# Four graph layers on one core: the last group's output projection by pairs, and a new order for its last full step

## The chip, the cores and the metric

The kernel runs on one core of a Trainium2 chip. The metric is the device time of one execution in microseconds. The core has TensorE (PE in the profile, with its weight loads as PEld), VectorE (DVE), ScalarE (ACT), GpSimd (POOL) and SyncE (SP), whose queue issues nearly all of the DMA transfers here.

## The reference

128 graphs of 64 nodes, each node with 512 features, pass through four layers. Each layer has the form `x = layernorm(x + f(x))`. All is float32.

```python
# layer 0: hypergraph convolution twice, with H = (adj != 0)
h = layer_norm(relu(hypergraph_conv(x, adj, W1, b1)), gamma, beta)      # 512 -> 1024
x = _layernorm(x + hypergraph_conv(h, adj, W2, b2) + x)                 # 1024 -> 512
# layer 1: additive attention weights A from s = x @ w @ a
x = _layernorm(x + A @ x @ w)
# layer 2: three graph convolutions  adj @ (x @ W) + b
x = _layernorm(x + gcn(relu(gcn(relu(gcn(x, W1, b1)), W2, b2)), W3, b3))
# layer 3: 8 heads of 64, softmax over the 64 nodes, plus adj and exp(-adj)
attn = softmax(q @ k.T * scale, masked) * 0.33 + 0.33 * adj + 0.33 * exp(-adj)
x = _layernorm(x + (attn @ v) @ W_out + b_out)
```

What follows concerns the end of layer 3: the softmax, `attn @ v`, the projection by `W_out`, and the last layer norm.

## The kernel before, in words

**Tiling.** Two graphs make a pair of 128 rows; four pairs make a group of 512 rows (`G = 4`), two pairs a duo. There are 16 groups (`NGRP`). A group's rows stay in the tile `x` (128 partitions, 4 pairs, 512 features) through all four layers.

**Products.** A product of 512x512 by 512x512 is done in blocks of 256 by Strassen's scheme in Winograd's form. `multiply` (L516) issues seven block products through `product` (L498), each four matmuls of 128x256, so 28 instead of 32. The left side is a `Left` object (L474), whose `sums` (L484) adds up four blocks on DVE; the right side needs seven blocks of the weight, three of them as given and four made once and kept in DRAM. `Stream` (L331) loads them through SP into a ring of 20 slots, one block at a time, in the order of use. Accumulators are `a_`, `b_` and `c_` with the name of the product; they, `pv` and the accumulators of plain products share four PSUM buffers. Between products ACT copies `u_` out (L524), or DVE adds the residual to it (L526), and DVE adds the results (L544, L548, L552); the last block is copied by ACT (L555) or added by DVE (L557).

**Plain products.** `rows_of` (L803), inside the first group's function, does it without Strassen: for one pair, eight matmuls of 128x256 into one accumulator.

**Layer 3** is the end of `second_half` (L980). `scores` (L1107) makes the dots `dot` and their scaled and masked form `sm`; `softmax` (L1140) works on `sm` in place, for each duo and each half `h2` of the heads: maximum, subtraction, exp on ACT, sum, reciprocal, multiplication. `turn_probs` (L1153) transposes `sm` into `ptp`, and adds the adjacency part to make `pt`. `attend` (L1175) multiplies by `v` into `pv`, which ACT copies into the left side `oT`. Then come `oT`'s sums, the product `wo`, `layer_norm` (L435) and the store. In the last group the norm and the store are made in two halves, of two pairs each.

**Order.** Three groups are in flight: the first half of one (`a`), the second half of the one before (`b`), and the tail of the one before that (`t`, from `v` on). Step by step, the list `order` (L1205) says which part is emitted next; a part that no group has at that step is left out. So step 16 has only `b` of group 15 and `t` of group 14, and step 17 only `t` of group 15:

```python
    order = """
        t.v1 a.c1 t.v b.gt t.soft a.w1a1 a.w1a t.soft2 a.resid b.l2a1 b.l2a a.w1b1 t.ptp a.w1b t.pv a.lnh t.osum
        b.l2b1 a.c2a b.l2b a.c2b b.gb3 load a.w21 b.gh a.w2 rows b.l2c1 b.l2c2 a.ss b.l2c t.o1 a.den t.o2 a.c3 b.agg t.o
        a.p1 b.xT a.p2 b.q1 b.q t.ln3 b.k1 prep b.k b.dots
    """.split()
```

A trailing digit is a stop inside a product (`v1` is after its third block product, `o1` after the first, `o2` after the third). `gt` is the graph product ahead of layer 2, `l2a`, `l2b`, `l2c` are layer 2's products, `agg` its last aggregation, `xT` the transposes `xtp` ahead of layer 3.

A scheduler then orders each engine's instructions, and may move one ahead of others that were written before it. Two things bind it. `behind(key)` (L471) keeps instructions after a given addition on DVE. And an `Engine` wrapper (L119) puts each instruction after the one written before it on the same engine, while `opening[0]` is true, which it is in the first group's list `start` only.

Of the kernel before, what the change touches and what calls it, by code (L numbers as in the profile page):

```python
# [8 lines left out]
FP = mybir.dt.float32  # L9
U8 = mybir.dt.uint8  # L10
AF = mybir.ActivationFunctionType
ALU = mybir.AluOpType
AX = mybir.AxisListType

P = 128
C = 64
D = 512
DH = 1024
HEADS = 8
G = 4  # L20
T = G * P
KD = D // P
Q = 256
# [18 lines left out]
def kernel(  # L42
# [71 lines left out]
    PE, DVE, ACT, POOL, SP = (  # L114
        getattr(mybir.EngineType, n) for n in ("PE", "DVE", "Activation", "Pool", "SP")
    )
    opening = [False]

    class Engine:  # L119

# [3 lines left out]

        def __getattr__(self, name):
            op = getattr(self.engine, name)
            if not opening[0]:
                return op

            def call(*args, **kwargs):  # L130
                with in_turn(self.kind):
                    return op(*args, **kwargs)

            return call
# [90 lines left out]
    class Weight:  # L225
# [17 lines left out]
                nc.sync.dma_start(out=t, in_=self.kept[u][what])  # L243
            return t

        def load_quads(self):
            quads = []
            for u in range(self.halves):
                b = {}
                for k, n in ((0, 0), (1, 0), (0, 1), (1, 1)):  # L250
                    b[k, n] = self.tile(f"b{k}{n}", 0, u)
                    nc.sync.dma_start(out=b[k, n], in_=self.quad_src(u, k, n))
                quads.append(b)
            return quads
# [76 lines left out]
    class Stream:  # L331


        def __init__(self, uses):
            self.todo = []
            for wt, q in uses:
                if q == 0:
                    self.todo.append((wt, q, None, 8))
                else:
                    self.todo += [(wt, q, what, wt.halves) for what in ORDER]  # L340
            self.here = {}
            self.held = 0
            self.to_make = {}
            self.uses = uses

        def pump(self):
            while self.todo and self.held + self.todo[0][3] <= RING:
                wt, q, what, n = self.todo.pop(0)
                self.held += n
                if q > 0:  # L350
                    self.here[wt, q, what] = [wt.load(q, what, u) for u in range(wt.halves)]
                elif wt in by_pairs:
                    by_pairs[wt] = None if wt.scaled else wt.load_quads()
                else:
                    self.to_make[wt] = wt.load_quads()
# [65 lines left out]
    def bcast(t, n):  # L421

        return t.unsqueeze(2).to_broadcast([P, n, C])
# [47 lines left out]
    def behind(key):  # L471
        return tc.issue_after(last_add[key]) if key in last_add else nullcontext()
# [25 lines left out]
    def product(acc, lefts, wt_q, what, first, last, flipped):  # L498
        ws = stream.take(*wt_q, what)
        n_k = 2 * len(lefts)  # L500
        for blk in range(2):
            for i in range(n_k):
                left, wt = lefts[i // 2].left[what][:, i % 2], ws[i // 2][:, i % 2]
                if flipped:
                    lhsT, rhs = wt[:, blk * P : (blk + 1) * P], left
                else:
                    lhsT, rhs = left[:, blk * P : (blk + 1) * P], wt

                ten.matmul(  # L509
                    acc[:, blk, :], lhsT, rhs,  # L510
                    start=(first and blk == 0 and i == 0), stop=(last and i == n_k - 1),
                    skip_group_check=True,
                )
        stream.done(*wt_q, what)

    def multiply(lefts, wt_q, dst, key, flipped=False, res=None, stops=(3,)):  # L516


        acc = [ps_acc.tile([P, 2, Q], FP, name=f"{n}_{key}", tag="acc") for n in "ab"]

        def snap(ps, m, n, what):
            t = work.tile([P, 2, Q], FP, name=f"{what}_{key}", tag="w")
            if res is None:
                act.copy(t, ps)  # L524
            else:
                vec.tensor_add(t, ps, res(m, n))  # L526
            return t

        pa, pc = acc
        product(pa, lefts, wt_q, B11, True, False, flipped)  # L530
        s1 = snap(pa, 0, 0, "u1")
        if 1 in stops:
            yield
        product(pc, lefts, wt_q, T1, True, False, flipped)
        s5 = snap(pc, 1, 1, "u5")
        if 2 in stops:
            yield
        product(pa, lefts, wt_q, T2, False, False, flipped)
        s2 = snap(pa, 0, 1, "u2")
        if 3 in stops:  # L540
            yield
        pb = ps_acc.tile([P, 2, Q], FP, name=f"c_{key}", tag="acc")
        product(pb, lefts, wt_q, B21, True, True, flipped)
        vec.tensor_add(dst(0, 0), pb, s1)  # L544
        if 4 in stops:
            yield
        product(pa, lefts, wt_q, T3, False, False, flipped)
        vec.tensor_add(dst(1, 1), pa, s5)  # L548
        if 5 in stops:
            yield  # L550
        product(pc, lefts, wt_q, B22, False, True, flipped)
        last_add[key] = vec.tensor_add(dst(0, 1), pc, s2).ins  # L552
        product(pa, lefts, wt_q, T4, False, True, flipped)
        if res is None:
            act.copy(dst(1, 0), pa)  # L555
        else:
            vec.tensor_add(dst(1, 0), pa, res(1, 0))  # L557

    def whole(gen):
        for _ in gen:  # L560
            pass

    def nat(t):

        return lambda m, n: t[:, 2 * m : 2 * m + 2, n * Q : (n + 1) * Q]
# [225 lines left out]
    def constant(g):  # L791
        for p in range(G):
            vec.scalar_tensor_tensor(
                g["x"][:, p, :], bw_bc, g["cs"][:, p : p + 1], g["x"][:, p, :], ALU.mult, ALU.add
            )

    def first_group(g):


        q, xg = g["q"], g["x"]  # L800
        pair = lambda p: xg[:, p, :]

        def rows_of(p, ts, quads, u0=0, u1=None, ps=None):  # L803

            if ps is None:
                ps = ps_acc.tile([P, 2, Q], FP, name=f"pp_{p}", tag="acc")
            us = range(len(ts))[u0:u1]
            for n in range(2):
                for u in us:
                    for c in range(KD):  # L810
                        ten.matmul(
                            ps[:, n, :], ts[u][:, c, p * P : (p + 1) * P], quads[u][c // 2, n][:, c % 2],
                            start=(n == 0 and u == 0 and c == 0), stop=(u == len(ts) - 1 and c == KD - 1),
                            skip_group_check=True,
                        )
            return ps

        def stats(mv, st, at, src):
            vec.bn_stats(st, src)
# [160 lines left out]
    def second_half(g):  # L980
# [94 lines left out]
        probs = [scores(g, duo, qT, kT) for duo in range(2)]  # L1075
        yield "dots"
        v = big.tile([P, G, D], FP, name=f"v_{q}", tag="big")
        for _ in multiply([left], (w_v, q), nat(v), f"v_{q}"):
            yield "v1"
        yield "v"  # L1080
# [1 line left out]
        with behind(f"v_{q}"):  # L1082
            softmax(g, 1, probs[1], (0,))
        yield "soft"
        with behind(f"l0w10_{q + 2}"):
            softmax(g, 1, probs[1], (1,))
        yield "soft2"
        pts = [turn_probs(g, duo, probs[duo]) for duo in range(2)]
# [9 lines left out]
        yield "o"  # L1098
        with behind(f"q_{q + 1}"):
            o = out[q * T : (q + 1) * T, :].rearrange("(p t) d -> t p d", t=P)  # L1100
            for pairs in (range(G),) if q < NGRP - 1 else (range(2), range(2, G)):
                layer_norm(xg, f"l3_{q}_{pairs[0]}", pairs)
                at = slice(pairs[0], pairs[-1] + 1)
                nc.sync.dma_start(out=o[:, at], in_=xg[:, at])
        yield "ln3"

    def scores(g, duo, qT, kT):  # L1107

# [29 lines left out]
        return ds  # L1138

    def softmax(g, duo, ds, h2s):  # L1140

        for h2 in h2s:
            d, key = ds[h2], f"{g['q']}_{duo}_{h2}"
            mx = small.tile([P, 8], FP, name=f"mx_{key}", tag="mx")
            vec.reduce_max(mx, d, axis=AX.X)
            vec.tensor_sub(d, d, bcast(mx, 8))
            act.activation(d, d, AF.Exp)
            sm = small.tile([P, 8], FP, name=f"sum_{key}", tag="sum")
            vec.reduce_sum(sm, d, axis=AX.X)
            vec.reciprocal(sm, sm)  # L1150
            vec.tensor_mul(d, d, bcast(sm, 8))

    def turn_probs(g, duo, probs):  # L1153

# [20 lines left out]
    def attend(g, duo, pts, v, left):  # L1175
# [36 lines left out]
        b.l2a1 b.l2a a.lnh b.l2b1 a.c2a b.l2b a.c2b b.gb3 load a.w21 b.gh a.w2 b.l2c1 sumsq b.l2c2 a.ss b.l2c a.den b.agg  # L1212
        a.c3 a.p1 b.xT sumsk a.p2 b.q1 b.q b.k1 rows b.k prep b.dots
    """.split()
    lag = {"a": 0, "b": 1, "t": 2}
    todo = []
    for what in start:
# [6 lines left out]
            todo.append((what, 0, None))  # L1224
    n_start = len(todo)
    for step in range(1, NGRP + 2):
        for what in order if step > 1 else step_1:
            who, dot, name = what.partition(".")
            key = (who, step - lag[who], name) if dot else (what, step + 1, None)
            if 0 <= key[1] < NGRP and key not in todo:  # L1230
                todo.append(key)
    used = {
        ("a", "w1a"): w_1[0], ("a", "w1b"): w_1[1], ("a", "w2"): w_2, ("a", "p2"): w_l1, ("b", "l2a"): w_g[0],
        ("b", "l2b"): w_g[1], ("b", "l2c"): w_g[2], ("b", "q"): w_q, ("b", "k"): w_k, ("t", "v"): w_v,
# [6 lines left out]
        if wt is not None:  # L1241
            uses.append((wt, q))
    stream = Stream(uses)
    opening[0] = True
    groups, gens, preps = {0: first}, {}, {0: prepare(first)}
    next(preps[0])
    next(preps[0])
# [3 lines left out]
        w_2.load_raw()  # L1251
    scaling, bw_parts = w_2.scale(), w_2.beta_times()
    for n, (who, q, name) in enumerate(todo):
        opening[0] = n < n_start
        if who == "load":
            if q > 1:
                groups[q] = load_group(q)
# [98 lines left out]
```

## Time and profile before

| | us |
|---|---|
| median of three runs (2805.82 to 2807.02) | 2805.87 |
| the profiled execution | 2804.13 |
| its span, first to last instruction | 2802.3 |
| PE busy | 2769.3 (99%) |
| DVE busy | 2003.7 (72%) |
| ACT busy | 818.2 (29%) |
| step 16, from group 14's `dot` to group 15's | 2651.84 to 2758.06 |
| last group's `v` begins | 2760.09 |
| last matmul begins, end of its modelled run | 2793.3, 2793.68 |

The granted TensorE clock is 0.999 over the whole span. Matmuls are pipelined and their ends are modelled, so starts say more than durations; a busy PE is not a PE at its peak. The profiled execution lies 1.74 us under the median. In a row of the timeline, the time in brackets is what the engine stood idle before, with what ended the wait.

### The profile page before, as it was taken

What the parts mean: (1) busy time and instruction counts of PE and PEld (TensorE: products, weight loads), DVE (VectorE), ACT (ScalarE), POOL (GpSimd) and SP (SyncE); (2) the same over time, 40 slices, a digit from 0 to 9 for tenths busy, and PEclk for the clock granted to TensorE, in tenths of its full rate; (3) what the DMA queues carried; (4) which work ended last, traced back from release to release, by engine and by line L of the source; (5) the groups of instructions that cost most, each with busy time, mean ns of one, the idle gap of its engine ahead of it and who ended that gap; (6) DMA issues with size and microseconds to landing.
All of it is one profiled execution on the core that took longest, in us unless ns stands there. A gap on an engine that the chain in (4) does not pass through costs nothing.

```text
span 2802.3 us, 67764 instructions
## 1 busy us (share of the span) xinstructions
PE 2769.3 (99%) x28862; PEld 2362.0 (84%) x28862; DVE 2003.7 (72%) x3861; ACT 818.2 (29%) x1467; POOL 38.1 (1%) x72
## 2 busy tenths in 40 slices
PE   9999999999999999999999999999999999999998
PEld 7878888888888888888888888888888888888877
DVE  6768677676776767767677776767767677676756
ACT  3223323232232322322233232232323223232222
POOL 2000000000000000000000000000000000000000
PEclk9999999999999999999999999999999999999999
DMA  8444454454544545445454454545545454454541
GB/s 259 165 127 148 130 158 140 139 162 131 165 129 136 163 129 166 127 142 163 133 158 130 142 160 128 162 129 150 152 133 162 130 158 135 132 162 129 147 118 64
DMA packets 309660, 405.94 MB, mean 145 GB/s; under 512 B 57424, under 2 KB 184944, under 8 KB 309360
## 3 DMA queue, kind: packets, MB, share of 16 engines
q1 hardware_dynamic: 304384, 385.84, 46.5%
q0 software_dynamic: 4976, 15.76, 1.5%
q8 instruction: 229, 3.75, 0.5%
q14 instruction: 71, 0.58, 0.1%
HBM read 370.57 MB, written 30.93 MB: 143 GB/s over the span
## 4 chain that ended last, share of the span: by engine, by line
PE 86%; DVE 8%; ACT 1%; issue 0%; DVEq 0%
PE a_l0w L509 13%; PE b_l0w L509 7%; PE a_l2b L509 4%; PE a_q L509 4%; PE a_k L509 4%; PE a_v L509 4%; PE c_l0w L509 4%; PE a_l2a L509 4%; PE a_l1w L509 4%; PE gt_l L458 3%; PE a_wo L509 3%; PE a_l2c L509 2%; PE gt_l0h L458 2%; PE b_l1w L509 2%; PE b_v L509 2%; PE b_l2b L509 2%
## 5 line engine op out<-in xcount | busy, mean ns | idle before, releaser
L509 PE MATMUL a_l0w<-w2w,aT_l0h 128*128 128x256 f32 x720 | 164.3, 381 | 0.0
L440 DVE BATCH_NORM_STATS2 st_l<-x 128x6 f32<-128x512 f32 x248 | 160.2, 674 | 0.1
L509 PEld LDWEIGHTS a_l0w<-w2w,aT_l0h 128*128 128x128 f32 x720 | 135.6, 190 | 18.8
L696 ACT ACTIVATE h<-h 128x1024 f32<-128x1024 f32 x58 | 61.3, 1057 | 216.6 <-DVE h L552 195.0
L444 DVE TENSOR_SCALAR x<-x,mv_l,rs_l 128x512 f32<-128x512 f32 x248 | 120.1, 542 | 1.8
L466 ACT COPY aT_l<-gt_l 128x512 f32<-128x512 f32 x176 | 90.5, 600 | 71.1 <-PE gt_l L458 71.0
L509 PE MATMUL b_l0w<-w2w,s_l0h 128*128 128x256 f32 x480 | 108.5, 379 | 0.0
L509 PEld LDWEIGHTS b_l0w<-w2w,s_l0h 128*128 128x128 f32 x480 | 90.1, 190 | 13.5
L1023 ACT ACTIVATE aT_h<-gth,gb_col 128x256 f32<-128x256 f32 x128 | 48.4, 489 | 159.0 <-PE gth L1015 159.0
L431 ACT ACTIVATE rs_l<-mv_l,eps_t 128x4 f32<-128x4 f32 (+1 forms) x63 | 18.8, 298 | 258.1 <-DVE mv_l L441 256.8
L509 PE MATMUL a_l2b<-gwbw,aT_h 128*128 128x256 f32 x360 | 86.9, 384 | 4.7 <-ACT aT_oT L1195 4.7
L509 PE MATMUL a_l2a<-aT_l,gwaw 128*128 128x256 f32 x360 | 86.6, 383 | 1.0 <-ACT aT_l L466 1.0
L509 PE MATMUL a_q<-aT_xT,wqw 128*128 128x256 f32 x360 | 86.6, 383 | 0.2 <-ACT aT_xT L1062 0.2
L509 PE MATMUL a_v<-wvw,aT_xT 128*128 128x256 f32 x360 | 86.6, 383 | 0.0
L509 PE MATMUL a_l2c<-gwcw,aT_h 128*128 128x256 f32 x360 | 85.3, 380 | 0.6 <-DVE g L548 0.6
L509 PE MATMUL a_wo<-wow,aT_oT 128*128 128x256 f32 x360 | 85.3, 380 | 0.0
L509 PE MATMUL a_l1w<-ww,aT_l 128*128 128x256 f32 x360 | 85.1, 379 | 0.0
L509 PE MATMUL a_k<-aT_xT,wkw 128*128 128x256 f32 x360 | 85.0, 379 | 0.0
L509 PE MATMUL a_l0w<-w1aw,aT_l 128*128 128x256 f32 x336 | 82.3, 388 | 0.0
L509 PE MATMUL a_l0w<-w1bw,aT_l 128*128 128x256 f32 x336 | 81.7, 379 | 0.0
L526 DVE TENSOR_TENSOR u_l0w<-a_l0w,b_bc 128x512 f32<-128x512 f32 x56 | 38.5, 688 | 59.8 <-PE a_l0w L509 59.8
L509 PEld LDWEIGHTS a_l2b<-gwbw,aT_h 128*128 128x128 f32 x360 | 67.1, 190 | 15.2 <-ACT aT_oT L1195 6.6
(503 smaller groups left out, 6464.5 us busy)
## 6 DMA issues: line engine op xcount, KB each, us to landing
w2w<-w2k SPq DMA_DIRECT2D x210, 256.0 KB, 2.7
x<-in_x_dram SPq DMA_DIRECT2D x15, 1024.0 KB, 6.3
w1aw<-w1ak SPq DMA_DIRECT2D x60, 256.0 KB, 2.7
w1bw<-w1bk SPq DMA_DIRECT2D x60, 256.0 KB, 2.7
ww<-wk SPq DMA_DIRECT2D x60, 256.0 KB, 2.7
gwaw<-gwak SPq DMA_DIRECT2D x60, 256.0 KB, 3.7
gwbw<-gwbk SPq DMA_DIRECT2D x60, 256.0 KB, 2.7
gwcw<-gwck SPq DMA_DIRECT2D x60, 256.0 KB, 2.7
```

The lines of the kernel that those rows point to most:

```text
L431: act.activation(rs[:, at], mv[:, at, 1], AF.Sqrt, bias=eps_t)
L440: vec.bn_stats(st, xg[:, p, :])
L444: vec.tensor_scalar(xg[:, p, :], xg[:, p, :], mv[:, p, 0:1], rs[:, p : p + 1], ALU.subtract, ALU.mult)
L458: ten.matmul(ps[g][f * C : (f + 1) * C, c, p, :], src(2 * duo + p)[rows, c0 : c0 + C], mat[rows, 2 * duo + p, :], start=True, stop=True,)
L466: act.copy(o[:, :, :, g, :], ps[g])
L509: ten.matmul(acc[:, blk, :], lhsT, rhs, start=(first and blk == 0 and i == 0), stop=(last and i == n_k - 1), skip_group_check=True,)
L526: vec.tensor_add(t, ps, res(m, n))
L696: act.activation(hn, hn, AF.Relu)
L1023: act.activation(o[:, :, h, :], ps[h][:, c].rearrange("p (d a) i -> p d (a i)", d=2), AF.Relu, bias=gb2_col[:, k : k + 1],)
```

## The change

**The last full step.** Step 16 gets a list of its own, `step_last`, and step 17 another, `rest_last`. In `step_last`, `b.gt` stands between the two parts of `t.v`, `t.ptp` between the two parts of `b.l2a`, and `b.agg` ahead of `t.o2`. The second half of the softmax of group 14 is kept behind the last addition of its `v`.

**The last group.** `last_rows` takes the place of the tail for group 15. The projection is plain, with `rows_of` moved outward so that both can call it, and with the four given blocks of `W_out`, loaded together. Each pair is added to `x`, normalised and stored by itself; the last pair is added in two half rows, each with its statistics. `ptp` of duo 0 goes ahead of the seventh block product of `v`; `pv` of duo 0, the projection of pair 0, `ptp` of duo 1, half of pair 1, `pv` of duo 1, the other half, and pairs 2 and 3 follow. The softmax is split into `softmax_steps` and issued in written order. From the last group's `v` on, PE and DVE keep the written order (`strict`); ACT does not.

```diff
@@ Stream
                 if q == 0:
                     self.todo.append((wt, q, None, 8))
+                elif (wt, q) == (w_o, NGRP - 1):
+                    self.todo.append((wt, q, None, 4))
...
-                if q > 0:
+                if what is None and q > 0:
+                    self.here[wt, q] = wt.load_quads(q)
+                elif q > 0:
@@ multiply
         last_add[key] = vec.tensor_add(dst(0, 1), pc, s2).ins
+        if 6 in stops:
+            yield
         product(pa, lefts, wt_q, T4, False, True, flipped)
@@ second_half
         v = big.tile([P, G, D], FP, name=f"v_{q}", tag="big")
+        if q == NGRP - 1:
+            yield from last_rows(g, probs, v, left)
+            return
...
-        with behind(f"l0w10_{q + 2}"):
+        with behind(f"l0w10_{q + 2}" if q < NGRP - 2 else f"v_{q}"):
             softmax(g, 1, probs[1], (1,))
...
-            for pairs in (range(G),) if q < NGRP - 1 else (range(2), range(2, G)):
-                layer_norm(xg, f"l3_{q}_{pairs[0]}", pairs)
-                at = slice(pairs[0], pairs[-1] + 1)
-                nc.sync.dma_start(out=o[:, at], in_=xg[:, at])
+            layer_norm(xg, f"l3_{q}")
+            nc.sync.dma_start(out=o, in_=xg)
         yield "ln3"
+
+    def last_rows(g, probs, v, left):
+
+        q, xg = g["q"], g["x"]
+        o = out[q * T : (q + 1) * T, :].rearrange("(p t) d -> t p d", t=P)
+        gen = multiply([left], (w_v, q), nat(v), f"v_{q}", stops=(3, 6))
+        next(gen)
+        yield "v1"
+        steps = [[softmax_steps(g, duo, probs[duo], h2) for h2 in range(2)] for duo in range(2)]
+        for n in range(2):
+            for h2 in range(2):
+                next(steps[0][h2])
+        for n in range(2):
+            next(steps[1][0])
+        for h2 in range(2):
+            next(steps[0][h2])
+        next(gen)
+        yield "v2"
+        left = Left(f"oT_{q}")
+        pts = turn_probs(g, 0, probs[0])
+        whole(gen)
+        yield "v"
+        attend(g, 0, pts, v, left)
+        for n in range(2):
+            next(steps[1][1])
+        for h2 in range(2):
+            next(steps[1][h2])
+        yield "pv0"
+
+        def projected(p, ps=None, n=None):
+            return rows_of(p, [left.t], stream.here[w_o, q], ps=ps, ns=range(2) if n is None else (n,))
+
+        def added(p, ps, n=None):
+            cols = slice(0, D) if n is None else slice(n * Q, (n + 1) * Q)
+            row = xg[:, p, cols]
+            vec.tensor_add(row, ps.rearrange("p n f -> p (n f)")[:, cols], row)
+
+        def written(p):
+            layer_norm(xg, f"l3_{q}_{p}", (p,))
+            nc.sync.dma_start(out=o[:, p], in_=xg[:, p])
+
+        ps = projected(0)
+        pts = turn_probs(g, 1, probs[1])
+        added(0, ps)
+        written(0)
+        yield "o1"
+        ps = projected(1, n=0)
+        attend(g, 1, pts, v, left)
+        ps = projected(1, ps, n=1)
+        added(1, ps)
+        written(1)
+        yield "pv1"
+        added(2, projected(2))
+        written(2)
+
+        st = small.tile([P, 2, 6], FP, name="st_last", tag="st_last", bufs=1)
+        ps = None
+        for n in range(2):
+            ps = projected(3, ps, n=n)
+            added(3, ps, n)
+            vec.bn_stats(st[:, n], xg[:, 3, n * Q : (n + 1) * Q])
+        mv = small.tile([P, 1, 2], FP, name="mv_last", tag="mv_last", bufs=1)
+        vec.bn_aggr(mv[:, 0, :], st.rearrange("p n s -> p (n s)"))
+        rs = rstd(mv, 1, "last")
+        vec.tensor_scalar(xg[:, 3], xg[:, 3], mv[:, 0, 0:1], rs[:, 0:1], ALU.subtract, ALU.mult)
+        nc.sync.dma_start(out=o[:, 3], in_=xg[:, 3])
+        yield "o"
+
+    def softmax_steps(g, duo, ds, h2):
+
+        d, key = ds[h2], f"{g['q']}_{duo}_{h2}"
+        mx = small.tile([P, 8], FP, name=f"mx_{key}", tag="mx")
+        vec.reduce_max(mx, d, axis=AX.X)
+        yield
+        vec.tensor_sub(d, d, bcast(mx, 8))
+        act.activation(d, d, AF.Exp)
+        yield
+        sm = small.tile([P, 8], FP, name=f"sum_{key}", tag="sum")
+        vec.reduce_sum(sm, d, axis=AX.X)
+        vec.reciprocal(sm, sm)
+        vec.tensor_mul(d, d, bcast(sm, 8))
+        yield
@@ the lists of steps
+    step_last = """
+        t.v1 b.gt t.v t.soft t.soft2 b.l2a1 t.ptp b.l2a t.pv t.osum b.l2b1 b.l2b b.gb3 b.gh b.l2c1 b.l2c2 b.l2c t.o1 b.agg
+        t.o2 t.o b.xT b.q1 b.q t.ln3 b.k1 b.k b.dots
+    """.split()
+    rest_last = "t.v1 t.v2 t.v t.pv0 t.o1 t.pv1 t.o".split()
+    orders = {1: step_1, NGRP: step_last, NGRP + 1: rest_last}
...
+        if n == n_start:
+            strict.clear()
+        if n == n_end:
+            strict.update((PE, DVE))
```

More of the change, by code (lines that the diff above doesn't have):

```diff
@@ L116 @@
     )
-    opening = [False]
+    strict = set()
     class Engine:
@@ L126, in __getattr__ @@
             op = getattr(self.engine, name)
-            if not opening[0]:
+            if self.kind not in strict:
                 return op
@@ L244, in load, with load_quads @@
             return t
-        def load_quads(self):
+        def load_quads(self, q=0):
             quads = []
@@ L250, in load_quads @@
                 for k, n in ((0, 0), (1, 0), (0, 1), (1, 1)):
-                    b[k, n] = self.tile(f"b{k}{n}", 0, u)
+                    b[k, n] = self.tile(f"b{k}{n}", q, u)
                     nc.sync.dma_start(out=b[k, n], in_=self.quad_src(u, k, n))
@@ L795, in constant, with rows_of @@
             )
+    def rows_of(p, ts, quads, u0=0, u1=None, ps=None, ns=range(2)):
+        if ps is None:
+            ps = ps_acc.tile([P, 2, Q], FP, name=f"pp_{p}", tag="acc")
+        us = range(len(ts))[u0:u1]
+        for n in ns:
+            for u in us:
+                for c in range(KD):
+                    ten.matmul(
+                        ps[:, n, :], ts[u][:, c, p * P : (p + 1) * P], quads[u][c // 2, n][:, c % 2],
+                        start=(n == 0 and u == 0 and c == 0), stop=(u == len(ts) - 1 and c == KD - 1),
+                        skip_group_check=True,
+                    )
+        return ps
     def first_group(g):
@@ L801, in first_group @@
         pair = lambda p: xg[:, p, :]
[L803 to L816, printed above, removed]
         def stats(mv, st, at, src):
@@ L1142, in softmax @@
         for h2 in h2s:
[L1143 to L1151, printed above, removed]
+            whole(softmax_steps(g, duo, ds, h2))
     def turn_probs(g, duo, probs):
@@ L1226 @@
     for step in range(1, NGRP + 2):
-        for what in order if step > 1 else step_1:
+        for what in orders.get(step, order):
             who, dot, name = what.partition(".")
@@ L1231 @@
                 todo.append(key)
+    n_end = todo.index(("t", NGRP - 1, "v1"))
     used = {
@@ L1243 @@
     stream = Stream(uses)
-    opening[0] = True
+    strict.update((PE, DVE, ACT))
     groups, gens, preps = {0: first}, {}, {0: prepare(first)}
@@ L1253 @@
     for n, (who, q, name) in enumerate(todo):
-        opening[0] = n < n_start
+        if n == n_start:
+            strict.clear()
+        if n == n_end:
+            strict.update((PE, DVE))
         if who == "load":
```

## The prediction

> **What bounds the kernel now.** I read the page first. One row says who is the bound over the whole span:
>
> ```profile
> PE 2769.3 (99%) x28862; PEld 2362.0 (84%) x28862; DVE 2003.7 (72%) x3861; ACT 818.2 (29%) x1467; POOL 38.1 (1%) x72
> ```
>
> TensorE is busy 99%. A change gains only where TensorE stands still, or after its last matmul. The instruction orders of the two kernels are the same, names aside, up to step 16 (the last in which two groups overlap), so all that counts lies after about 2650 us. For that stretch I read the chain of waits; each piece that is not PE is time in which TensorE had nothing to do:
>
> ```profile
> 2668.27 0.97 ACT aT_l L466 x2
> ...
> 2687.37 0.61 DVE pt L1169
> ...
> 2731.37 0.47 DVE x L444
> ...
> 2771.44 1.19 DVE mx L1145 x2
> ...
> 2792.71 1.29 DVE st_l L440 x2
> ...
> 2797.33 0.55 DVE x L444
> ```
>
> Five holes: the evictions of gt_l before l2a; the pt additions that hold pv; the layer norm that holds the transposes xtp; the second softmax (from mx) in the last group; and the whole norm at the end. The timeline of PE gives the places, and what TensorE waited for in brackets:
>
> ```profile
> 2669.28 1.99 PE L509 MATMUL a_l2a<-aT_l,gwaw 128*128 128x256 f32 x8 [1.04 <-ACT aT_l L466]
> ...
> 2731.88 1.57 PE L1057 MATMUL xtp<-identc,x 64*128 64x64 f32 x30 [1.03 <-DVE x L444]
> ...
> 2776.51 1.29 PE L1162 MATMUL ptp<-identc,sm 64*128 64x64 f32 x16 [1.67 <-DVE sm L1151]
> 2777.73 3.17 PE L1186 MATMUL pv<-pt,v 64*64 64x64 f32 x120
> ```
>
> A product of four matmuls (x8: two records each) starts every 1.727 us; a block of 128 records of 64x64 takes 2.02 us (dot, 2758.06 to 2760.09). So pv at 3.17 us for 120 is slow. The granted clock in half-microseconds says why:
>
> ```profile
> 2776.50:2777.00 0.50, 0.46 (x8) 0.32 (x8) 0.50 (x2) 0.00 (x0) 0.00 (x0) 1.00 0.00 0
> 2777.00:2777.50 0.50, 0.39 (x8) 0.39 (x8) 0.50 (x2) 0.00 (x0) 0.00 (x0) 0.50 0.00 0
> ```
>
> The column before the DMA share is the clock: it halves at 2777.0, after 3.4 us in which TensorE was almost idle, and comes back at about 2780.4. Last, the stores, in the list of DMA issues (size and time to landing):
>
> ```profile
> out_dram<-x SPq DMA_DIRECT2D x1, 1024.0 KB, 4.2
> out_dram<-x SPq DMA_DIRECT2D x2, 512.0 KB, 2.9
> ```
>
> **The change, step 16.** From dot at 2651.84 to dot at 2758.06, before takes 106.2 us.
>
> (a) gt goes from behind v to between v's third and fourth product. The work is the same 2.02 us with one way in and out of small tiles as before, but its four copies on ACT (2.03 us) and the four sums on DVE (4 x 0.6) now run under four products. l2a starts directly: 1.0 us gained. What goes late is the second half of the softmax: v's last add moves from 2664.53 to about 2666.75, so sm is ready at about 2673.3.
>
> (b) The 32 transposes ptp go into l2a after its third product, due 2673.5, so sm just makes it. Slack 0.2 us; each 0.1 us that DVE is later costs as much. The pt additions (4 x 0.6 us) then run under l2a's second half. Before, PE took from the end of l2a (2681.88) to b_l2b (2689.54) for ptp, pv and one product of l2b: 7.66 us. After: l2a ends at 2681.8, now with ptp inside. pv still waits for a PSUM slot, freed by the copy of a_l2a on ACT, which stands behind two relu of 0.66 us: 2682.85. Then 2.02 + 0.1 for pv, 1.83 for the first product of l2b, so b_l2b at 2686.88 against 2689.54. With (a) that is 2.66 us, my figure up to here.
>
> (c) agg goes ahead two products of wo. It waits for nothing (g is written 0.6 us into a_wo). It puts 4 additions and the norm of group 15 on DVE 3.45 us earlier; ending at about 2726.5 against TensorE's arrival at 2727.7, they no longer hold xtp (1.03 us), nor its first copies. The wait of the last product on x L548 (0.2) goes too, but u_wo, now behind the norm's work on DVE, holds the fourth product for about 0.2. Sum: a_q at 2729.65 against 2733.69, or **4.0 us** for the step. Groups 14 and 15 use the same weights in the same order; the SP queue is unchanged but for wo's loads, four instead of seven, waiting for four free slots at once: at about 2747 instead of 2737 to 2748, and needed 28 us later. They stand ahead of group 14's store, whose data are ready at 2752.5. Cost nothing; were they 28 us late, every microsecond more would count.
>
> **The change, last group.** I keep the old clock, as if v began at 2760.09.
>
> Work: wo by pairs is 32 matmuls of 128x256 instead of 28: 4 x 0.432 = 1.73 us more on TensorE. Six more ways in and out of small tiles at about 0.1 (a_v after dot is 1.83 and not 1.73): 0.6 more. Against that the Strassen sums (4 x 0.6) and three u_wo leave DVE.
>
> The chain in the written order: sum_01 waits for its exp until 2766.87, mul ends 2768.5; v's adds follow their products to 2771.46. ptp0 runs at 2770.64 (0.6), v's last product to 2773.1, its copy on ACT to 2773.95. pv0 2774.0 to 2775.15 (hole 0.9); its copies, two in 1.09, to 2776.28 (hole 1.2). DVE meanwhile: pt0, then the rest of softmax 1, ending at 2777.1. pp0 2776.3 to 2779.9; ptp1 to 2780.55; half of pp1 to 2782.4; pv1 (pt1 at 2782.0) to 2783.6; the other half to 2785.43. Here is the added wait: on ACT the square root of pair 0 stands ahead of pv1's copies. It waits for x<-pp0, which on DVE stands behind pt1: add 2781.9, statistics 0.72, aggregate 0.17, root to 2783.8, copies to 2784.95. pp2 needs them at 2785.43, so 0.5 us spare. pp2 to 2788.9, pp3 to 2792.35, last result at 2792.5; before, 2793.68.
>
> After that: DVE adds half a row (128x256: the 0.42 of L654's shape; bounds 0.2 and 0.69), statistics of it 0.4 (no row; between 0.17 of an aggregate and 0.67 of the full row), aggregate 0.2, root 0.3, reciprocal 0.15, scale 0.55, with gaps: the last scale ends at 2794.85. Before, the scale of 2797.33 is the first of two (1.00 us together) and ends the work at 2798.33: 3.5 us later. The store: 256 KB instead of 512, with nothing queued ahead. 1024 and 512 KB land in 4.2 and 2.9, so 1.3 for 512 KB, and 256 KB by the line 2.25 (upper bound 2.7, the page's median for w2w loads of that size, in traffic). Gain 0.65, bounds 0.2 and 1.0. Tail: 3.5 + 0.7 = **4.2 us**.
>
> [...] between 2773.1 and 2777.0 before did 0.34 + 0.46 us of matmuls. The trace dipped all the same, at some 24% busy. After, the worst 3.4 us (2772.9 to 2776.3) is some 38% busy. [...] by the row's measure a dip is possible[...], and 3.4 us at half speed under pp0 cost 1.7, leaving 6.5. I take no dip, as step 16 has stretches of 67% without one[...].
>
> **Sum.** 4.0 + 4.2 = 8.2 us. The profiled execution took 2804.13 (span 2802.3 and 1.8 around it), so 2795.9 for such a one; the median 2805.87 stands 1.74 higher and goes to **2797.7**.
>
> **The rivals.**
> Main case, 0.60: its own range 2796.0 to 2799.5, from the store's bounds (0.5 each way), the slack of 0.2 at ptp, and switches at 0 to 0.2 each.
> Dip of 3.4 us in the last group, 0.18: 2799.4. For it, the trace's dip at 24%; against, 38% and more.
> One half doesn't pay, 0.17: the gaps of step 16 return elsewhere (softmax 1 late at ptp, u_wo late at T3), or strict order makes DVE or ACT late by the 0.2 and 0.5 us of slack and more. Against: DVE's chain per pair (add, statistics, aggregate, root, reciprocal, scale) is 2.95 us against 3.45 of matmuls. Time: 2805.87 - 4.1 = 2801.8, which is within 0.2%.
> Slower, 0.03: the clock halves at pp0 and stays low to the end. From 2776.3 on there are 15.4 us of matmuls; at half speed each low microsecond costs 0.5, so 16 us of low clock eat the 8.2. All of it low: 2805.87 - 8.2 + 15.4 x 1.0 = 2813. Against: [...] pp is dense.
> The change doesn't do what it says, 0.02: the orders show the moves on each engine as described, so only a delayed wo load could undo it.
>
> 0.2% is 5.6 us, about what a measurement of this kernel can tell from no change. Faster by more: main and dip, and part of the third, 0.82; within: 0.14; slower by more: 0.04. The range reaches from the main case's better end, with a store at its best bound, to the third case: 2795.4 to 2801.9.
>
> **What would show it.** Right: a_l2a directly after v's seventh product; xtp without a wait; a_q about 4 us earlier against the first dot; in the tail holes of about 0.9 and 1.2 before pv0 and pp0, none before pp2; last matmul to end of span about 5.6 us instead of 8.6; clock 1.00 throughout the last group. Wrong: a clock of 0.50 under pp0, pp2 waiting for ACT's copies of pv1, ptp waiting for sm in l2a, or a last store that lands no sooner than 2.9 us.

## The result, and the profile after

The changed kernel takes 2797.61 us (median of seven runs, 2796.10 to 2800.23) against 2806.66 us before (seven runs, 2805.82 to 2807.03): a ratio of 0.997, 95% interval 0.9958 to 0.9982. The three runs of before that stood ahead of the prediction are among the seven. The profiled execution of the changed kernel took 2797.61 us, with a span of 2795.8.

The page's row of busy times is as good as unchanged. TensorE has eight records more (the four matmuls of the plain projection at two records each, 28870 against 28862), and what was gained is idle time:

```profile
PE 2769.4 (99%) x28870; PEld 2362.2 (84%) x28870; DVE 2000.2 (72%) x3858; ACT 818.3 (29%) x1469; POOL 38.1 (1%) x72
```

The chain of waits from 2640 us on shows which of the five holes are left. Columns: start, length, engine, what.

```profile
2669.74 1.73 PE a_l2a L513 x8
...
2685.38 0.49 ACT aT_oT L1275
...
2728.85 0.69 PE xtp L1063 x12
...
2771.63 0.98 ACT aT_oT L1275 x2
...
2787.64 0.89 DVE x L132 x2
2788.53 0.04 issue
2788.58 2.01 PE pp L132 x8
...
2792.30 0.55 DVE x L132
```

Before l2a and before xtp the chain now runs on PE without a break: the copies of gt_l and the norm of group 15 are off it. At 2685.38 the copies of pv appear where the additions of pt stood. At 2771.63 it is the copies of the first pv, where the second softmax stood. New is 2787.64: DVE's work on rows `x`, and after it a part of the projection `pp`. The timeline of PE says what that is:

```profile
2685.91 1.99 PE L513 MATMUL a_l2b<-gwbw,aT_h 128*128 128x256 f32 x8 [0.69 <-ACT aT_oT L1275]
...
2728.78 1.22 PE L1063 MATMUL xtp<-identc,x 64*128 64x64 f32 x32
...
2770.18 1.16 PE L132 MATMUL pv<-pt,v 64*64 64x64 f32 x64
2772.65 3.72 PE L132 MATMUL pp<-wob,aT_oT 128*128 128x256 f32 x16 [1.31 <-ACT aT_oT L1275]
...
2779.96 7.17 PE L132 MATMUL pp<-wob,aT_oT 128*128 128x256 f32 x32
2788.58 1.99 PE L132 MATMUL pp<-wob,aT_oT 128*128 128x256 f32 x8 [1.44 <-DVE x L132]
```

xtp has no wait in front. In the last group there is one hole of 1.31 us before pair 0's projection (`pp` at 2772.65), and one of 1.44 before the last four matmuls, which wait for DVE. The second is not in the prediction.

The clock (the column before the DMA share) stays at 1.00 to the last matmul, and a block of 64 records of pv takes 1.16 us. The row below is a stretch of 3.4 us around the first of these holes, and none around it has less than its 2.09 us of work on TensorE. Around the second hole, at the very end of the matmuls, a stretch of 3.4 us still holds 1.96:

```profile
2770.90:2774.30 3.40, 2.09 (x40) 1.77 (x32) 3.04 (x7) 2.88 (x4) 0.00 (x0) 1.00 0.00 0
```

The stores of one pair each, in the list of DMA issues from 2785 us on, land in 2.0 us, against 2.9 for two pairs:

```profile
out_dram<-x SPq DMA_DIRECT2D x3, 256.0 KB, 2.0
```

Where the time came from can be read off the starts in the timeline of PE, in one execution each. All in us; dot is that of group 14 at first, and v the last group's:

| stretch | before | after | gain |
|---|---|---|---|
| start of the span to group 14's dot | 2651.84 | 2653.14 | -1.30 |
| dot to a_l2a | 17.44 | 16.44 | 1.00 |
| a_l2a to b_l2b | 20.26 | 18.16 | 2.10 |
| b_l2b to a_q | 44.15 | 42.92 | 1.23 |
| a_q to group 15's dot | 24.37 | 24.37 | 0 |
| dot to v | 2.03 | 2.02 | 0.01 |
| v to the end of the span | 42.21 | 38.75 | 3.46 |

From group 14's dot on the change gains 7.8 us. All but 0.07 of the last group's 3.46 comes behind its last matmul, whose modelled end is 33.59 us after v's start in before and 33.52 in after; from there to the end of the span it is 8.62 and 5.23.

The first row has nothing to do with the change: the instruction orders are the same up to there, and the difference is there already at the first gt_l0h (44.00 and 45.39 us). It fits the clock at the start. The first 64 records of `pp` take 14.08 us in before and 15.01 in after, the next 64 take 13.98 in both, and the trace's first record of the full clock begins at 12.2 us in before and at 15.1 in after. Over the twelve profiled executions of this study group 14's dot starts between 2651.84 and 2654.48, so what lies ahead of it moves a run by 2.6 us. That is why all experiments below are read by stretches first, and by medians second.

### The profile page after: what moved, and what is told of

It is laid out like the page before. It is cut to its first block, busy times and chain, and to the rows that moved or that the text cites. A ratio compares the mean times of both kernels' runs of the same rounds, so it can differ in the third digit from the quotient of the medians.

```text
span 2795.8 us, 67769 instructions
## 1 busy us (share of the span) xinstructions
PE 2769.4 (99%) x28870; PEld 2362.2 (84%) x28870; DVE 2000.2 (72%) x3858; ACT 818.3 (29%) x1469; POOL 38.1 (1%) x72
## 4 chain that ended last, share of the span: by engine, by line
PE 86%; DVE 7%; issue 4%; ACT 1%; DMA 1%; POOL 0%; SPq 0%; DVEq 0%; POOLq 0%
PE a_l0w L513 13%; PE b_l0w L513 7%; PE a_l2b L513 4%; PE a_q L513 4%; PE a_k L513 4%; PE a_v L513 4%; PE c_l0w L513 4%; PE a_l2a L513 4%; PE a_l1w L513 4%; PE gt_l L462 3%; PE a_wo L513 3%; PE a_l2c L513 2%; PE gt_l0h L462 2%; PE b_l1w L513 2%; PE b_l2b L513 2%
## 5 line engine op out<-in xcount | busy, mean ns | idle before, releaser
L513 PE MATMUL a_v<-wvw,aT_xT 128*128 128x256 f32 x336 | 80.8, 383 | 0.0
L513 PE MATMUL a_wo<-wow,aT_oT 128*128 128x256 f32 x336 | 79.5, 379 | 0.1
```

What stands on the lines that cost most here:

```text
L513: ten.matmul(acc[:, blk, :], lhsT, rhs, start=(first and blk == 0 and i == 0), stop=(last and i == n_k - 1), skip_group_check=True,)
```

## The experiments

**Each half by itself.** e1_step_only keeps step 16's list and has the last group as before; e2_tail_only keeps the last group's new tail and has step 16 as before.

```diff
 e1_step_only, against the changed kernel
-        if q == NGRP - 1:
-            yield from last_rows(g, probs, v, left)
-            return
...
-    orders = {1: step_1, NGRP: step_last, NGRP + 1: rest_last}
+    orders = {1: step_1, NGRP: step_last}
...
-        if n == n_end:
-            strict.update((PE, DVE))
...
 e2_tail_only, against the changed kernel
-        with behind(f"l0w10_{q + 2}" if q < NGRP - 2 else f"v_{q}"):
+        with behind(f"l0w10_{q + 2}"):
...
-    orders = {1: step_1, NGRP: step_last, NGRP + 1: rest_last}
+    orders = {1: step_1, NGRP + 1: rest_last}
```

> Only step 16's new order; the last group as before (Strassen projection, norm and store in two halves, scheduler's order). Theory: the two halves of the change add up without touching each other. Step 16, from dot to dot, takes 101.9 us as in the changed kernel (106.2 before), and from the last group's v to the end 42.2 us as before; so about 4.3 us faster than before, near 2802.3. Rival, the halves depend on each other (what step 16 saves comes back as a later weight load or a late norm in the last group): v to the end over 43 us, total gain under 3. Rival, the gain of the change is in the opening of the run: dot of group 14 starts more than 2 us earlier here and step 16 is near 106.

> Only the last group's new tail; step 16 in the old order. Theory: v to the end of the span takes 38.75 us as in the changed kernel (42.2 before), step 16 106.2 as before; about 3.5 us faster than before, near 2803.2. Rival, the halves depend on each other: v to the end differs from 38.75 by more than 0.5 us.

Measured: e1 2801.55 us, ratio to before 0.9985 (0.9979 to 0.9992); e2 2802.37 us, ratio 0.9987 (0.9980 to 0.9993). These are medians of 21 runs each, and before, run beside them 41 times, took 2805.81: gains of 4.26 and 3.44 us, 7.70 together, which agrees with the 7.8 of the traces. Step 16 takes 101.90 in e1 and 106.24 in e2; v to the end 42.66 and 38.84. So the halves add up: each stretch has its new length with its own half of the change and its old one without. The rival, that one half gives back what the other gains, falls, and so does the one that puts the gain into the opening: in e1 dot of group 14 starts at 2653.92, later than before.

e1 also shows the old tail's clock once more. The row below is the 3.4 us ahead of its drop, in stretches of the same kind as above; the next is a stretch after it:

```profile
2769.55:2772.95 3.40, 1.64 (x27) 1.00 (x26) 3.40 (x7) 1.82 (x3) 0.00 (x0) 1.00 0.00 0
...
2775.00:2777.00 2.00, 2.00 (x64) 1.88 (x68) 1.70 (x3) 0.00 (x0) 0.00 (x0) 0.50 0.04 8
```

The clock fell to 0.50 with TensorE 48% busy in the 3.40 us ahead, and stayed there for 6.8 us, against 3.4 in before. Of the five runs with the old tail, e1 and e7, with 6.8 us of low clock, take longest from v to the end (42.66 and 42.87); the three with 3.4 us take 42.03 to 42.38.

**Each move of step 16 by itself**, on the kernel before, one execution each.

```diff
 e5_gt_only
-        t.v1 t.v b.gt t.soft t.soft2 b.l2a1 b.l2a t.ptp ...
+        t.v1 b.gt t.v t.soft t.soft2 b.l2a1 b.l2a t.ptp ...
 e6_ptp_only
-        ... b.l2a1 b.l2a t.ptp t.pv ...
+        ... b.l2a1 t.ptp b.l2a t.pv ...
-        with behind(f"l0w10_{q + 2}"):
+        with behind(f"l0w10_{q + 2}" if q != NGRP - 2 else f"v_{q}"):
 e7_agg_only
-        ... b.l2c t.o1 t.o2 b.agg t.o ...
+        ... b.l2c t.o1 b.agg t.o2 t.o ...
```

> Before, with one move in step 16: gt between v's third and fourth product. Theory: the move is worth the wait of l2a for the copies of gt_l, 1.0 us, wherever it is made: dot to l2a 16.4 us instead of 17.4, step 16 105.2 instead of 106.2. Rival, the three moves need each other: gt alone makes the softmax late, pv waits longer for its pt, and the step stays at 106 or over.

> Before, with one move in step 16: the transposes ptp inside l2a, and the second softmax of group 14 behind v's last addition. Theory: worth the holes before and inside pv; from the start of l2a to l2b's second product 18.2 us as in the changed kernel, instead of 20.3; step 16 104.1. Rival, without the earlier gt DVE is busy with gt's sums when pt is due, and part of it is lost: step 16 over 104.8.

> Before, with one move in step 16: agg ahead of wo's second product. Theory: worth 1.2 us between l2b's second product and q (42.9 instead of 44.15), the norm of group 15 being done when xtp is due; step 16 105.0. The sum of the three moves alone should then be the 4.3 us of all three together. Rival, they overlap: the sum is over 4.8 or under 3.8.

| | dot to a_l2a | a_l2a to b_l2b | b_l2b to a_q | step 16 |
|---|---|---|---|---|
| before | 17.44 | 20.26 | 44.15 | 106.22 |
| e5, gt | 16.44 | 19.75 | 44.16 | 104.72 |
| e6, ptp | 17.44 | 18.61 | 44.16 | 104.58 |
| e7, agg | 17.44 | 20.26 | 42.91 | 104.98 |
| all three | 16.44 | 18.16 | 42.92 | 101.89 |

Alone they gain 1.50, 1.64 and 1.24 us, 4.38 together, against 4.33 for all three: they don't need each other and don't overlap. The gt move brings 0.5 us more than its own wait. With gt early the scheduler no longer puts two transposes of ptp between l2a's first two products, as it did before. e6 misses the 18.2, and so the expected 104.1, for the same reason: its order still has those two transposes there. The total times of single executions (2805.41, 2803.86, 2804.53) say nothing at this size, with openings at 2654.48, 2653.46 and 2652.93 and tails of 42.38, 42.03 and 42.87.

**The new wait.** e3_two_tiles gives the two half rows of pair 3 a tile each.

```diff
     def rows_of(p, ts, quads, u0=0, u1=None, ps=None, ns=range(2)):
+        n0 = 0 if ps is not None else ns[0]
...
-                        start=(n == 0 and u == 0 and c == 0), ...
+                        start=(n == n0 and u == 0 and c == 0), ...
...
-            ps = projected(3, ps, n=n)
+            ps = projected(3, n=n)
```

> The changed kernel, with the two half rows of pair 3's projection in two accumulator tiles instead of one. Theory: the 1.44 us for which TensorE waits before the last four matmuls comes from the shared tile alone, as DVE's addition of the first half has to read it first. With two tiles the wait goes, the last addition starts at once after the last matmul, and the end comes 1.5 us earlier: v to the end 37.2 us, near 2796.1. Rival, a third accumulator is not free in time or DVE, still at pair 2's norm, is what the end hangs on: the wait stays or moves, gain under 0.5 us. Rival, clock: [...] it should stay 1.00 to the last matmul.

Measured: 2795.24 us (2794.76 to 2796.15), ratio to before 0.9963 (0.9950 to 0.9975); v to the end 37.07, that is 1.68 less. In the timeline of PE the last 40 records of `pp` run in one row, with no wait; in that of DVE (the second line) the last addition starts 0.04 us after their end at 2787.94:

```profile
2779.04 8.90 PE L132 MATMUL pp<-wob,aT_oT 128*128 128x256 f32 x40
...
2787.98 0.42 DVE L132 TENSOR_TENSOR x<-pp,x 128x256 f32<-128x256 f32 x1
```

So the shared tile made the wait of 1.44 us: while DVE had yet to read one half of it, TensorE was kept from writing the other. Both rivals fall: a further accumulator was free in time, and the clock stayed at 1.00 to the last matmul (mean of the run 1.000; the 40 records take 8.90 us, 1.73 more than 32 in the changed kernel).

**The written order.** e4_free_order leaves PE and DVE in the last group to the scheduler; e10_pe_order keeps the written order on PE alone.

```diff
 e4_free_order
-        if n == n_end:
-            strict.update((PE, DVE))
 e10_pe_order
-            strict.update((PE, DVE))
+            strict.update((PE,))
```

> The changed kernel without the written order on PE and DVE in the last group: the scheduler orders it. It puts ptp of duo 1 ahead of the projection of pair 0, and the whole of pair 1 ahead of pv of duo 1. Theory: the written order lets pair 0's matmuls run under the second softmax; in the free order PE waits for that softmax to end (about 1.7 us more after the copies of pv0) before pp0, so v to the end is 1.5 to 2.5 us longer than 38.75 and the total near 2799.5. Rival, the written order is worth nothing, since the same pieces are there: within 0.5 us of the changed kernel. Rival, TensorE's longer hole halves the clock: it shows as 0.50 over 3.4 us and costs 1.7 us more.

> The changed kernel with the written order on PE alone; the scheduler orders DVE. Theory: of the 1.24 us, 0.92 is DVE's place for the half row's addition: the wait before the last four matmuls is about 0.5 us, and v to the end 37.8 to 38.3, some of it lost as the additions to ptp of duo 1 now stand behind pair 0's addition and statistics. Rival, PE's order is what counts: the wait stays at 1.4, v to the end 38.75.

Measured: e4 2797.15 us (2795.04 to 2798.02), ratio to before 0.9968 (0.9955 to 0.9980), v to the end 37.51. My theory had the wrong sign: by v to the end, the written order costs 1.24 us. (The medians, 2797.15 here and 2797.61 for the changed kernel, lie too close to tell.) Two rows of e4's timeline of PE show the two places:

```profile
2772.10 5.45 PE L811 MATMUL pp<-wob,aT_oT 128*128 128x256 f32 x24 [0.55 <-ACT aT_oT L1275]
...
2786.26 1.99 PE L811 MATMUL pp<-wob,aT_oT 128*128 128x256 f32 x8 [0.52 <-DVE x L1148]
```

The scheduler fills DVE's gaps with the second softmax, and has it done in time for the transposes of duo 1 to run in the hole before pair 0 (0.55 left of 1.31). Late in the group it adds pair 3's first half row ahead of pair 2's scale, so the wait on the shared tile is 0.52 and not 1.44.

e10, one execution, has the second of these (the wait is 0.52) and not the first: v to the end 38.43, slightly above what I expected. Of the 0.92 us gained at the wait 0.6 is lost again, and not where I expected it. Here are e10's rows of PE around pv of duo 0, and of DVE the additions for it:

```profile
2771.25 0.34 PE L132 MATMUL pv<-pt,v 64*64 64x64 f32 x8
2771.85 1.04 PE L132 MATMUL pv<-pt,v 64*64 64x64 f32 x56 [0.25 <-DVE pt L1249]
2774.08 3.72 PE L132 MATMUL pp<-wob,aT_oT 128*128 128x256 f32 x16 [1.19 <-ACT aT_oT L1275]
...
2770.51 1.28 DVE L1249 TENSOR_TENSOR pt<-ptp,adt 128x512 f32<-128x512 f32 x2
```

The scheduler has put more of the softmax ahead of v's addition and of these additions, so pv waits inside for `pt`, and pair 0's projection begins 16.11 us after v's start instead of 15.60. That is 0.51 of the 0.6. The additions for duo 1, which do stand behind pair 0's addition and statistics, cost only the other 0.09. In e4 pair 0 begins at 16.11 too, but the transposes of duo 1 are then already done.

**Further.** e8_fill adds to e3 one more move in step 16: wo's first product ahead of l2c. e9_fill_free is e8 in the scheduler's order.

```diff
-        ... b.gb3 b.gh b.l2c1 b.l2c2 b.l2c t.o1 b.agg t.o2 t.o b.xT ...
+        ... b.gb3 b.gh t.o1 b.l2c1 b.l2c2 b.l2c t.o2 b.agg t.o b.xT ...
-        ... f"wo_{q}", res=nat(xg), stops=(1, 3))):
+        ... f"wo_{q}", res=nat(xg), stops=(1, 3) if q != NGRP - 2 else (1, 2))):
```

> The two-tile kernel, with one move more in step 16: wo's first product goes ahead of l2c, and agg behind wo's second product. Theory: TensorE stands still for 1.03 us before l2c's second product while DVE adds up the left side; a product that needs nothing of it fills that: step 16 100.9 instead of 101.9, total 1.0 us under the two-tile kernel. Rival, accumulators: wo's accumulator stays open through l2c, and with four PSUM buffers one of l2c's products waits: step 16 unchanged or longer. Rival, agg comes one product nearer to xtp and the norm holds it again, up to 1 us: no gain.

> The kernel with two tiles and wo's first product ahead of l2c, and the scheduler's order in the last group instead of the written one. Theory: the free order of the changed kernel was faster by 1.24 us mainly because DVE added the first half row of pair 3 before pair 2's scale, so the wait on the shared tile was 0.52 instead of 1.44; with two tiles that wait is gone in either order, and order is worth under 0.3 us: v to the end 37.0 against 37.08, total within 0.5 us of the fill kernel. Rival, the free order gains by itself, ptp of duo 1 filling the hole before pp0: v to the end under 36.5.

Measured: e8 2794.32 us (2793.75 to 2795.01), ratio to before 0.9961 (0.9947 to 0.9975); e9 2794.08 us (2793.18 to 2795.30), ratio 0.9957 (0.9943 to 0.9971). Both lie below the changed kernel; each was run against before, and not against the other. Step 16 is 100.48, which is 1.41 less and more than the 1.0 expected. The first two products of l2c, in the changed kernel and (the lower two rows) in e8:

```profile
2700.73 2.00 PE L513 MATMUL a_l2c<-gwcw,aT_h 128*128 128x256 f32 x8
2703.77 1.97 PE L513 MATMUL b_l2c<-gwcw,s_h 128*128 128x256 f32 x8 [1.03 <-issue]
...
2702.34 1.89 PE L513 MATMUL a_l2c<-gwcw,aT_h 128*128 128x256 f32 x8
2704.07 1.89 PE L513 MATMUL b_l2c<-gwcw,s_h 128*128 128x256 f32 x8
```

From start to start they are 1.73 us apart instead of 3.04, so the gap was worth 1.31 and not the 1.03 in brackets, which is counted from a modelled end. Most of the rest is at wo's fifth product, which starts 1.82 us after the fourth instead of 1.95. The norm of group 15 ends 0.4 us after xtp has begun, but xtp does not wait. The rival of the accumulators does not show. Between e8 and e9 the tail differs by 0.36 us (37.08 and 36.72), in e9's favour, so order is worth a little more than the 0.3 I allowed and far less than the 1.24 it was with the shared tile. The rival's 36.5 is not reached either.

## Why the prediction was right

The forecast was 2797.7 us, 8.2 below before, with 4.0 from step 16 and 4.2 from the last group. The traces show 4.33 and 3.46, 7.8 together; the two misses partly cancel. That the median came within 0.1 us of the forecast is luck: it moved by 9.05, the seven runs spread over 4.1, and the stretch ahead of step 16 alone moves a run by 2.6.

**(a)** Expected 1.0 for the copies of gt_l, measured 1.00.

**(b)** Expected 1.66 for ptp (1.74 if the terms are added as written, to 2686.80), measured 2.10. The term that was mis-sized is the wait of pv for a PSUM slot, for which 1.05 us was set down. pv starts 1.82 us after l2a's last product, which is that product and one way into small tiles (from the last a_k to dot in before, 2650.02 to 2651.84, it is 1.82 too): no wait. The wait is one place later, 0.69 us before l2b, for the copies of pv (the row of l2b stands above):

```profile
2681.28 1.89 PE L513 MATMUL a_l2a<-aT_l,gwaw 128*128 128x256 f32 x8
2683.10 2.12 PE L1266 MATMUL pv<-pt,v 64*64 64x64 f32 x128
```

The two transposes that no longer split l2a are in this figure too, 0.5 us by e5.

**(c)** Expected 1.38 (4.04 less 2.66), measured 1.23. xtp follows wo without a wait, as said, and all of the gain lies between xtp's start and a_q (3.12 us before, 1.88 after). The predicted 0.2 us for u_wo came one product later than said: wo's fifth product, and not the fourth, starts 1.95 us after the one before it instead of 1.73. It uses up the 0.2 us that the last product no longer waits.

**The last group**, in us from the start of v (the prediction's figures less 2760.09):

| | predicted | after | e3, two tiles |
|---|---|---|---|
| pv of duo 0 starts | 13.9 | 13.13 | 13.13 |
| pair 0's projection starts | 16.2 | 15.60 | 15.60 |
| last matmul's modelled end | 32.4 | 33.52 | 31.81 |
| last scale ends | 34.8 | 35.80 | 34.09 |
| span ends | 38.0 | 38.75 | 37.07 |

The prediction's hole of 0.9 before pv was not there: v's last block product fills only rows of pairs 2 and 3, and duo 0 needs pairs 0 and 1 (pv starts at 2770.18, ACT's copy of that product at 2770.29). The hole before pair 0 was there, 1.31 us for the predicted 1.2. The copies of the second pv, behind pair 0's square root on ACT, did not hold pair 2, as predicted: they end at 2781.18, and pair 2 begins about 2781.8.

The step that failed is "pp2 to 2788.9, pp3 to 2792.35": it took pair 3's two halves as one run of matmuls. The second half waited 1.44 us for DVE to have read the first out of the same tile, and before that DVE had pair 2's scale to do:

```profile
2787.64 0.55 DVE L132 TENSOR_SCALAR x<-x,mv_l,rs_l 128x512 f32<-128x512 f32 x1
2788.10 0.42 DVE L132 TENSOR_TENSOR x<-pp,x 128x256 f32<-128x256 f32 x1
```

So the last matmul ends at 33.52 where 32.4 was predicted, and of the 1.2 us by which it was to end earlier than in before (33.59) almost nothing is left. e3 takes the wait away, and then it ends at 31.81, 0.6 before the prediction, by what pv gained.

What follows is as predicted or better: from the last matmul to the last scale 2.28 us (2.35), statistics of a half row 0.43 (0.4), and from the last scale to the end of the span 2.95 instead of 3.97. The store is the second term that was mis-sized: 1.02 us gained, where I took 0.65 and gave 1.0 as the bound. A line through 1024 and 512 KB gave 2.25 us for 256 KB; it landed in 2.0.

**The clock.** No dip came, as taken, but not for the reason given. With the holes as predicted the worst 3.4 us would have been 38% busy, and in e5 and e7 the clock fell after 3.40 us that were 31% and 41% busy (1.06 and 1.38 us of matmuls). It was the missing hole before pv that left 61%. That part of the forecast was luck: the old tail dipped in all five kernels that have it (before, e1, e5, e6, e7), with TensorE 11% to 48% busy in the 3.40 us ahead (last section).

**The rivals.** "One half doesn't pay" is refuted by e1 and e2. "Slower" needed 16 us of low clock, and there was none. What no run separates is the pieces of the last group's gain: e2 tests the new tail only as a whole, and the shares of the shorter norm, the smaller store and the clock are read from the traces.

## What to carry to other kernels

When one engine is busy 99%, look for the gain in the last step of a pipeline, where there is nothing left to fill its waits: moving work that is ready into a product which doesn't need it was worth its waits to within half a microsecond here, and each move could be priced by itself. Where the result of a product is taken out by halves, give each half a tile of its own, and ask of every product what must have read its tile first: here the half that was meant to overlap waited 1.44 us. An order written out by hand should be run against the scheduler's; here it lost 1.24 us with the shared tile, and 0.36 without.

## What the runs showed of the hardware that was not expected

TensorE's granted clock dropped to 0.50 while the engine was at work. It did so in the last group of each of the five kernels with the old tail, in one execution each. The busy times are those of TensorE, all in us:

| | clock falls at | busy in the 3.40 us ahead | busy in the first 3.4 us at 0.50 | time at 0.50 |
|---|---|---|---|---|
| before | 2777.0 | 0.80 (24%) | 3.3 | 3.4 |
| e1 | 2773.0 | 1.64 (48%) | 2.1 | 6.8 |
| e5 | 2778.5 | 1.06 (31%) | 3.3 | 3.4 |
| e6 | 2776.5 | 0.36 (11%) | 3.4 | 3.4 |
| e7 | 2775.3 | 1.38 (41%) | 2.4 | 6.8 |

In before the clock returns to 1.00 at 2780.41 and falls again at 2797.48, 3.80 us behind the modelled end of the last matmul (2793.68). In the changed kernel it stays at 1.00 to the last matmul, and from 2640 us to there the emptiest 3.40 us hold 1.96 us of matmuls (58%). How much work keeps the clock, or brings it back, these traces don't show: no run was made to find it.

A store of 256 KB with nothing ahead of it landed in 2.0 us in the changed kernel; in before two of 512 KB, one right behind the other, took 2.9 (median of the two).
